# Inverse roots on ScalarE and GpSimd in place of GpSimd's power, and 175 more state products on GpSimd

## The chip, the cores and the metric

One core of one Trainium2 chip runs the whole program. The metric is device time in microseconds (us). The engines are called PE (TensorE, matrix products), PEld (its weight loads), DVE (VectorE), ACT (ScalarE), POOL (GpSimd) and SP (SyncE, which here only issues DMAs).

## The reference, cut to what matters

Eight images of 64 channels and 128 x 128 pixels go through two layers. The first is a filter of nine weights for each pixel, from a small convolution and a softmax. The second norms its input, runs two bidirectional selective-scan (Mamba) blocks over the 16,384 pixels as a sequence, multiplies the outcome with a convolved branch, norms again and ends in a gated feed-forward net (FFN). What the change touches are the norms and the scan:

```python
def layernorm(x, w, b):
    mu = x.mean(-1, keepdims=True)
    var = ((x - mu) ** 2).mean(-1, keepdims=True)
    return (x - mu) * jax.lax.rsqrt(var + EPS) * w + b

def rmsnorm(x, w):
    return x * jax.lax.rsqrt((x * x).mean(-1, keepdims=True) + EPS) * w

def selective_scan(u, dt, A, Bm, Cm, D, z):
    dt = jax.nn.softplus(dt)
    dA = jnp.exp(jnp.einsum('bdl,dn->bldn', dt, A))
    dBu = jnp.einsum('bdl,bnl,bdl->bldn', dt, Bm, u)
    ...                                    # h[l] = dA[l] * h[l-1] + dBu[l]
    y = jnp.einsum('bldn,bnl->bdl', hs, Cm) + D[None, :, None] * u
    return y * jax.nn.silu(z)
```

The state has 128 channels times 16 numbers, so 2048 rows of 16,384 steps for each direction of each block of each image.

## The kernel before, in words

The sequence is cut into chunks of 1024 steps: 16 chunks make a pass, and each image has four passes (two blocks, two directions), so there are 8 x 64 = 512 chunks. In each block the first direction is a **first pass** (it stores its output to DRAM) and the other a **second pass** (it adds the stored output, multiplies by the gate, projects, and norms the result for the next block). A chunk is 16 **steps**, u = 0 to 15; one step is one tile of 128 state rows by 1024.

In a step, ACT computes the decays `w` into PSUM (`decay`, L1097, two buffers), DVE scans them with the driving term `bu` (`scan`, L1115 and L1117), and the states are multiplied by `cp` to give `hs` (`product`). For an odd step this product is made by DVE (L1139); for an even one that `on_pool` names, DVE scans into `hs` directly and POOL multiplies in place (L1136). ACT copies the last column of the states for the next chunk (`keep`, L1129). POOL makes the driving terms two steps at a time (`drive`, L1089, three buffers) and one product for each chunk (`dtx`, L1045). PE sums the products over the state (`collect`, L1155). Softplus runs for a later chunk in step u = 2, Silu in step u = 11.

Beside the chunks run three other kinds of work on the same engines: the **front** (first layer and three norms of the next image, beside chunks 36 to 62 of an image), the **mix** (the convolved branch and a norm, beside chunk 62 and the first ten or so chunks of the next image) and the **FFN** (beside chunks 11 to 35 of the next image; three Gelus each in `gelus`, L853 and L855). "Plain" chunks have nothing beside them; they lie mostly in the first image. Before the first chunk stand two or so pieces of the first front alone, and after the last one a remainder of the last FFN.

A norm goes as follows. PE sums squares into 8 columns (`means`), ACT adds epsilon (`means_out`, L458), POOL raises to the power −0.5 (`root`, L461), PE spreads the result over the channels (`rb` in `spread`, L467), and DVE multiplies (`scaled`, `third_norm`, `normed`: L585, L617, L1201). There are 768 roots: three for each of 128 front pieces, one for each of 128 mix pieces, one for each of 256 second-pass chunks.

The order is written out by hand: `at(time, phase, function)` puts each piece of work at a step time and a phase (FEED, SCAN, MID, PROD, DECAY, REST), all are sorted by these two, and each engine takes its instructions in that order. The same phase keeps the order in which the pieces were planned: chunks first, then front, mix and FFN. For the norm that is:

```python
at(b + 13, DECAY, n.means_out)
at(b + 14, REST, n.root)
feed(b + 17, n.spread, mm_tile)
at(b + 18, DECAY, self.normed)
```

ACT holds one table of functions at a time. Exp, Silu, Softplus and Gelu need different ones; before the change each load stands directly ahead of the function that needs it.

Of the kernel before, what the change touches and what calls it, by code (L numbers as in the profile page):

```python
# [8 lines left out]
F32 = mybir.dt.float32  # L9
BF16 = mybir.dt.bfloat16  # L10
AF = mybir.ActivationFunctionType
ALU = mybir.AluOpType
# [3 lines left out]
P = 128  # L16
# [3 lines left out]
ROWS = 4  # L20
# [13 lines left out]
G = 4  # L34
U = G * G
PW = W + 2
FEED, SCAN, MID, PROD, DECAY, REST = range(6)

IMAGE = 4 * NT * U
# [16 lines left out]
def kernel(ctx: ExitStack, tc: tile.TileContext, a: dict, out: bass.AP):  # L56
# [6 lines left out]
    nc = tc.nc  # L63
# [8 lines left out]
    def const(shape, name, dt=F32):  # L72
        return wp.tile(shape, dt, tag=name, name=name)
# [3 lines left out]
    def dram(shape, name):  # L77
        return dramp.tile(shape, F32, tag=name, name=name + "_dram")


    def image(name):

        return dram([C, PW * PW + PW], name)

    def pixels(img):
        return img[:, 0 : PW * PW].rearrange("c (r w) -> c r w", w=PW)

    def clear(img, lo=0, hi=PW + 1):
        nc.sync.dma_start(
            img.rearrange("c (r w) -> c r w", w=PW)[:, lo:hi],  # L90
            zero.rearrange("c (o w) -> c o w", o=1).to_broadcast([C, hi - lo, PW]),
        )

    x_img, xm_img, xn_img = image("x"), image("xm"), image("xn")
    dw_img = [image(f"dw{i}") for i in range(2)]
    zero = const([C, PW], "zero")
    nc.vector.memset(zero, 0.0)
# [11 lines left out]
    nc.vector.tensor_tensor(center, center, ident, ALU.add)  # L109
    eps = const([P, 1], "eps")  # L110
    nc.vector.memset(eps, EPS)
    neg_half = const([P, 2 * ROWS], "neg_half")
    nc.vector.memset(neg_half, -0.5)

    sel_y = const([P, 32, 1], "sel_y")
    nc.vector.tensor_reduce(sel_y, ident.rearrange("k (m n) -> k m n", n=G), AX.X, ALU.add)
# [49 lines left out]
    for h in range(2):  # L166
        nc.sync.dma_start(b1[h * 32 : (h + 1) * 32, :], row(a["L0_conv_b1"]))
        nc.sync.dma_start(w2v[64:65, 9 * h : 9 * h + 9], a["L0_conv_b2"].rearrange("(o k) -> o k", o=1))


    FRONT_W, MIX_W, FFN_W = 6 * 32 + P, 12 * C, 18 * P + 2 * C + P + 2 * 9
    w_dram = [dram([P, n], f"w{i}") for i, n in enumerate((FRONT_W, MIX_W, FFN_W))]
# [210 lines left out]
    wk = ctx.enter_context(tc.tile_pool(name="wk", bufs=2))  # L383
# [19 lines left out]
    def tmp(name):  # L403
        return wk.tile([P, N], F32, tag="tmp", name=name, bufs=12)
# [41 lines left out]
    class Norm:  # L446
# [7 lines left out]
                )  # L454

        def means_out(self):
            self.r = wk.tile([P, 2 * ROWS], F32, tag="r", name="r", bufs=4)
            nc.scalar.activation(self.r, self.mp[:, 0 : 2 * ROWS], AF.Identity, bias=eps)  # L458

        def root(self):  # L460
            nc.gpsimd.tensor_tensor(self.r, self.r, neg_half, ALU.pow)  # L461

        def spread(self, ps):
            self.rb = ps("rb")
# [15 lines left out]
    class Front:  # L480
        def __init__(self, b, c):
            self.b, self.c, self.p = b, c, b % 2
            self.n1, self.n2, self.n3 = Norm(), Norm(), Norm()
            self.t, self.wbk, self.alone = {}, {}, False
# [278 lines left out]
    class Ffn:  # L763
# [84 lines left out]
        def gelus(self):  # L848
            if self.alone:
                nc.scalar.activation(self.gt, self.gt, AF.Gelu)  # L850
            else:
                self.gt = tmp("gt")
                nc.scalar.activation(self.gt, self.rest[0], AF.Gelu)  # L853
            for h in range(2):
                nc.scalar.activation(self.ga[h], self.ga[h], AF.Gelu)  # L855

        def rest_times(self):
            nc.vector.tensor_tensor(self.gt, self.gt, self.rest[1], ALU.mult)
# [33 lines left out]
        def plan(self, a):  # L892
            early = 12 if self.alone else 0
            at(a - 4 - early, REST, self.load, 0)
            at(a - 3 - early, REST, self.load, 1)

            if self.alone:
                at(a - 6, REST, self.before_taps)
                at(a - 5, DECAY, self.before_taps_out)
                at(a - 5, REST, self.taps, 0)  # L900
                at(a - 2, REST, self.taps, 1)
                groups = ((0, 0, self.first_out, 2), (3, 1, self.times, 6))
                gelus, out = 3, 9
            else:
                groups = ((0, 0, self.first_out, 5), (6, 2, None, 0), (14, 1, self.times, 19))
                gelus, out = GELU, 19
            for t, g, end, to in groups:
                for i in range(4):
                    at(a + t + (0 if self.alone else i), REST, self.conv, g, i)
                for h in range(2 if end else 0):  # L910
                    at(a + to, DECAY, end, h)
            at(a + gelus, REST, self.gelus)
            at(a + gelus + 2, MID, self.rest_times)
            at(a + out - 5, REST, self.load_x2)
            at(a + out, REST, self.project)
            at(a + out + 2, DECAY, self.add)
            at(a + out + 2, REST, self.store)

    def plan_ffn(b, a, step):
        at(a - (10 if step == LAST_FFN_STEP else 4), REST, load_weights, 2)  # L920
        for c in range(NCH):
            Ffn(b, c).plan(a + step * c)


    gelu_times = {IMAGE * b + FFN_AT + FFN_STEP * c + GELU for b in range(B - 1) for c in range(NCH)}
# [7 lines left out]
    class Chunk:  # L933


        def __init__(self, i):
            self.b, self.l, self.d, self.t, self.second = order[i]
            self.i, self.t0 = i, U * i
            self.first = i % NT == 0
            self.pairs = PAIRS[i % 2]  # L940
            r, last = self.t0 % IMAGE, self.b == B - 1
            self.beside_front = (
                FRONT_AT - FRONT_STEP <= r < FRONT_AT + NCH * FRONT_STEP + 16 and not last
            ) or self.t0 < FIRST_FRONT_AT + NCH * FRONT_STEP + 16
            self.beside_gelu = any(self.t0 - U <= t < self.t0 + 2 * U for t in gelu_times)
            self.prev = None
            self.bus, self.hss, self.ws = {}, {}, {}
            self.dup, self.dtp, self.bp, self.cp, self.yv = {}, {}, {}, {}, {}
            self.norm = Norm()
# [42 lines left out]
        def silu(self):  # L992
            nc.scalar.activation(self.xc, self.xc, AF.Silu)
            if self.second:
                nc.scalar.activation(self.gt, self.gt, AF.Silu)

        def store_gate(self):
            self.gt_d = sd.tile([DI, T], F32, tag="gate", name="gate_dram", bufs=4)
            nc.sync.dma_start(self.gt_d, self.gt)
            self.gt = {}  # L1000
# [18 lines left out]
        def softplus(self):  # L1019
            dt = self.dt  # L1020
            nc.scalar.activation(dt, dt, AF.Softplus)

        def bc(self):
            self.bcp = mm_tile("bcp")
            for i, s in enumerate(halves):
                nc.tensor.matmul(
                    self.bcp[32 * i : 32 * i + 32, :], wbc[:, self.l, self.d, :], self.xc[:, s],
                    start=True, stop=True,
                )
# [45 lines left out]
        def on_pool(self, u):  # L1075


            if u % 2 or u % 8 == 4 or self.t0 + u - 1 in gelu_times:
                return False
            return u != 8 or self.beside_front or self.beside_gelu  # L1080

        def over_pair(self, what, k):
# [217 lines left out]
    for b in range(B):  # L1300
# [2 lines left out]
        plan_mix(b, a + (LAST_MIX_AT if last else MIX_AT), LAST_MIX_STEP if last else MIX_STEP)  # L1303
        plan_ffn(b, a + (LAST_FFN_AT if last else FFN_AT), LAST_FFN_STEP if last else FFN_STEP)
    with tc.manual_schedule():
        for key in sorted(steps):
            for fn, args in steps[key]:
                fn(*args)
# [29 lines left out]
```

## Time and profile before

| what | value |
|---|---|
| three runs, median (lowest to highest) | 29515.6 us (29510.37 to 29532.13) |
| the profiled execution's own time | 29464.12 us |
| its span | 29462.3 us |
| POOL busy | 27653.4 us, 8732 instructions |
| DVE busy | 27280.7 us, 17559 instructions |
| ACT busy | 18566.1 us, 28357 instructions |
| PE busy | 23428.5 us, mean granted clock 0.866 |
| roots on POOL (L461) | 768, 1265.8 us |
| products on POOL (L1136) and on DVE (L1139) | 2832, 6693.9 us and 5360, 6562.4 us |

The profile takes one execution by the hardware profiler. Its groups give a line, an engine, an operation, output and inputs by the program's names, a count, the busy time and the mean duration of one, and then the idle time directly before these instructions with what ended it. A window gives each engine's busy time in a stretch of the span. The waits say which instruction waited for which, with total, number and longest.

### The profile page before, as it was taken

To read this page: it belongs to the slowest core of one execution; us is meant where nothing else is said; L and a number is where in the kernel's file an instruction comes from. 1 tells how busy PE (TensorE), PEld (TensorE's weight loads), DVE (VectorE), ACT (ScalarE), POOL (GpSimd) and SP (SyncE) were. 2 spreads that over 40 slices of the span, in tenths; PEclk is the share of its full clock that TensorE was granted. 3 is DMA by queue.
4 is the path that set the end of the run, shared out by engine and by line. 5 is a ranking of instruction groups with operands and counts; after the bars stand their busy time and mean duration, and the time that the engine had idled before them with its cause. 6 is when DMAs were issued, how large, how long until landed. Compare 5 with 4: busy or idle time off the path is not lost. (4 is left out here: it accounts for less than half of the span.)

```text
span 29462.3 us, 312607 instructions
## 1 busy us (share of the span) xinstructions
PE 23428.5 (80%) x97852; PEld 7363.8 (25%) x97852; DVE 27280.7 (93%) x17559; ACT 18566.1 (63%) x28357; POOL 27653.4 (94%) x8732
## 2 busy tenths in 40 slices
PE   7666888878788787887878878787787878878678
PEld 3211222223222232222322223222222222222123
DVE  4999999999999999999999999999999999999997
ACT  3666666666666666666666666666666666666663
POOL 3999999999999999999999999999999999999993
PEclk8777888988889888988889888898888988889789
DMA  4676677767777677776787767777677776777674
GB/s 114 221 245 219 226 246 242 240 217 230 249 241 237 216 234 254 239 233 217 235 256 235 233 219 237 251 239 229 221 239 247 236 228 219 246 246 238 217 250 142
DMA packets 2592281, 6762.83 MB, mean 230 GB/s; under 512 B 431270, under 2 KB 736822, under 8 KB 2589462
## 3 DMA queue, kind: packets, MB, share of 16 engines
q1 hardware_dynamic: 2590614, 6742.83, 70.7%
q8 instruction: 774, 12.68, 0.2%
q14 instruction: 893, 7.32, 0.1%
HBM read 5509.49 MB, written 1265.19 MB: 230 GB/s over the span
## 5 line engine op out<-in xcount | busy, mean ns | idle before, releaser
L1089 POOL TENSOR_TENSOR bu<-dup,bp 128x2048 f32<-128x2048 f32 x4096 | 18584.8, 4543 | 373.6 <-DVE w L1117 231.0
L1097 ACT ACTIVATE w<-dtp,a_neg 128x1024 f32<-128x1024 f32 x8192 | 9159.6, 1118 | 793.8 <-DVE hs L1115 334.7
L1136 POOL TENSOR_TENSOR hs<-hs,cp 128x1024 f32<-128x1024 f32 x2832 | 6693.9, 2364 | 236.0 <-ACT state L1129 183.1
L1139 DVE TENSOR_TENSOR hs<-w,cp 128x1024 f32<-128x1024 f32 x5360 | 6562.4, 1224 | 317.2 <-DMA cp<-bc_dram 88.5
L1117 DVE TENSOR_TENSOR_SCAN w<-w,state,bu 128x1024 f32<-128x1024 f32 x2683 | 6290.5, 2345 | 302.1 <-ACT w L1097 301.0
L1115 DVE TENSOR_TENSOR_SCAN w<-w,state,bu 128x1024 f32<-128x1024 f32 x2677 | 6278.7, 2345 | 250.2 <-ACT w L1097 248.8
L1155 PE MATMUL y<-hs,sel_y 128*32 128x512 f32 x32768 | 5126.6, 701 | 55.3 <-POOL hs L1136 55.1
L1129 ACT COPY state<-w 128x1 f32<-128x1 f32 x5360 | 838.0, 156 | 5484.9 <-DVE hs L1139 5433.5
L1117 DVE TENSOR_TENSOR_SCAN hs<-w,state,bu 128x1024 f32<-128x1024 f32 x1413 | 3308.4, 2341 | 183.3 <-issue 121.2
L1115 DVE TENSOR_TENSOR_SCAN hs<-w,state,bu 128x1024 f32<-128x1024 f32 x1419 | 3321.2, 2340 | 38.6 <-PE y L1155 17.5
L1148 PE MATMUL y<-xc,dskip 128*64 128x512 f32 x4096 | 1571.0, 856 | 1656.3 <-ACT yv L1172 1383.9
L967 PE MATMUL xp<-hn,wx 128*128 128x512 f32 x4096 | 2353.8, 704 | 653.6 <-ACT xc L973 476.2
L799 PE MATMUL fp<-fw,bgw 128*128 128x512 f32 (+1 forms) x5760 | 2272.1, 636 | 105.9 <-ACT ga L846 66.2
L1129 ACT COPY state<-hs 128x1 f32<-128x1 f32 x2832 | 541.2, 191 | 1937.8 <-DVE hs L1117 989.9
L1155 PEld LDWEIGHTS y<-hs,sel_y 128*32 128x32 f32 x32768 | 730.1, 117 | 3666.8 <-issue 2458.0
L1008 PE MATMUL dp<-xc,wdt 128*128 128x512 f32 x2048 | 1226.9, 683 | 463.8 <-ACT dt L1015 373.0
L461 POOL TENSOR_TENSOR r<-r,neg_half 128x8 f32<-128x8 f32 x768 | 1265.8, 1649 | 318.2 <-ACT r L458 299.2
L1097 ACT ACT_TABLE_LOAD x1134 | 1454.9, 1283 | 20.5
L566 PE MATMUL acc<-t,ident 128*128 128x512 f32 x2304 | 1370.9, 680 | 99.3 <-DVE hc L585 94.7
L805 PE MATMUL fp<-fw,bgw 64*128 64x512 f32 (+1 forms) x5760 | 1415.1, 609 | 0.0
L1045 POOL TENSOR_TENSOR dt<-dt,xc 128x1024 f32<-128x1024 f32 x512 | 1214.9, 2373 | 173.2 <-DMA dt_dram<-dt 154.7
L967 PEld LDWEIGHTS xp<-hn,wx 128*128 128x128 f32 x4096 | 830.6, 216 | 1967.7 <-issue 961.4
(211 smaller groups left out, 25729.1 us busy)
## 6 DMA issues: line engine op xcount, KB each, us to landing
bp<-bc_dram SPq DMA_DIRECT2D x4096, 256.0 KB
dup<-du_dram SPq DMA_DIRECT2D x4096, 256.0 KB
dtp<-dt_dram SPq DMA_DIRECT2D x4096, 256.0 KB
cp<-bc_dram SPq DMA_DIRECT2D x4096, 256.0 KB
hn<-hn_dram SPq DMA_DIRECT2D x1024, 256.5 KB
dt_dram<-dt SPq DMA_DIRECT2D x512, 512.0 KB
du_dram<-dt SPq DMA_DIRECT2D x512, 512.0 KB
yf_dram<-yv SPq DMA_DIRECT2D x512, 256.0 KB
```

The lines of the kernel that those rows point to most:

```text
L799: nc.tensor.matmul(o, wpair[:, i, g, m], self.win[h][:, i : i + ROWS, 0:W], start=(i == 0), stop=False)
L805: nc.tensor.matmul(o, wlast[rows, i, g, m], self.win[h][rows, i : i + ROWS, lo : W + lo], start=False, stop=(i == 2),)
L967: nc.tensor.matmul(self.xp[h], wx[:, self.l, self.d, i, :], self.hn2[:, s.start + 2 * i : s.stop + 2 * i], start=(i == 0), stop=(i == 1),)
L1089: nc.gpsimd.tensor_tensor(bu, self.dup[self.pairs[k][1]], self.over_pair("bp", k), ALU.mult)
L1097: nc.scalar.activation(w, self.dtp[gp][:, i, :], AF.Exp, scale=a_neg[:, self.l, self.d, g, j : j + 1])
L1115: nc.vector.tensor_tensor_scan(to, w, bu, s0, ALU.mult, ALU.add)
L1117: nc.vector.tensor_tensor_scan(to[:, ::-1], w[:, ::-1], bu[:, ::-1], s0, ALU.mult, ALU.add)
L1129: nc.scalar.copy(self.column(u), h[:, T - 1 : T] if self.d == 0 else h[:, 0:1])
L1136: nc.gpsimd.tensor_tensor(hs, hs, c, ALU.mult)
L1139: nc.vector.tensor_tensor(hs, w, c, ALU.mult)
L1148: nc.tensor.matmul(self.y[C * h : C * h + C, :], dskip[:, self.l, self.d, C * gp : C * gp + C], self.xc[:, s], start=True, stop=False,)
L1155: nc.tensor.matmul(self.y[lo : lo + 32, :], sel_y, hs[:, i, s], start=False, stop=(k % 4 == 3))
```

## The change

The mean of squares plus epsilon, v, is no longer raised to −0.5 by POOL. ACT computes r = exp(−0.5 ln v), v itself by Identity, and q = r squared. POOL makes one Newton step in three instructions, r (1.5 − 0.5 q v). So that Ln and Exp need no switch of tables between them, one table with both is loaded at the start and directly after every Silu, Softplus and (outside the last image) Gelu, rather than ahead of the next Exp. And `on_pool` names more steps: u = 4 in second-pass chunks beside a front, and in chunks beside an FFN without a Gelu directly ahead of u = 0 or 8.

```diff
+EXP_AND_LN = "natural_log_exp_and_others"
...
-    neg_half = const([P, 2 * ROWS], "neg_half")
-    nc.vector.memset(neg_half, -0.5)
...
+    def exp_and_ln():
+        nc.scalar.preload_act_table_set(EXP_AND_LN)
...
         def means_out(self):
-            self.r = wk.tile([P, 2 * ROWS], F32, tag="r", name="r", bufs=4)
-            nc.scalar.activation(self.r, self.mp[:, 0 : 2 * ROWS], AF.Identity, bias=eps)
+            mp, shape = self.mp[:, 0 : 2 * ROWS], [P, 2 * ROWS]
+            self.v, self.r, self.q = [wk.tile(shape, F32, tag=n, name=n, bufs=4) for n in ("rv", "r", "rq")]
+            nc.scalar.activation(self.r, mp, AF.Ln, bias=eps)
+            nc.scalar.activation(self.v, mp, AF.Identity, bias=eps)
+            nc.scalar.activation(self.r, self.r, AF.Exp, scale=-0.5)
+            nc.scalar.activation(self.q, self.r, AF.Square)

         def root(self):
-            nc.gpsimd.tensor_tensor(self.r, self.r, neg_half, ALU.pow)
+            nc.gpsimd.tensor_tensor(self.q, self.q, self.v, ALU.mult)
+            nc.gpsimd.tensor_scalar(self.q, self.q, -0.5, 1.5, ALU.mult, ALU.add)
+            nc.gpsimd.tensor_tensor(self.r, self.r, self.q, ALU.mult)
...
             for h in range(2):
                 nc.scalar.activation(self.ga[h], self.ga[h], AF.Gelu)
+            if not self.alone:
+                exp_and_ln()
...
+            self.skips = any(self.t0 + u - 1 in gelu_times for u in (0, 8))
...
             if self.second:
                 nc.scalar.activation(self.gt, self.gt, AF.Silu)
+            exp_and_ln()
...
             nc.scalar.activation(dt, dt, AF.Softplus)
+            exp_and_ln()
...
         def on_pool(self, u):
-            if u % 2 or u % 8 == 4 or self.t0 + u - 1 in gelu_times:
+            if u % 2 or u == 12 or self.t0 + u - 1 in gelu_times:
                 return False
+            if u == 4:
+                return self.beside_front and self.second or self.beside_gelu and not self.skips
             return u != 8 or self.beside_front or self.beside_gelu
...
     with tc.manual_schedule():
+        exp_and_ln()
         for key in sorted(steps):
```

## The prediction

> **What bounds the kernel now.** I read the busy line first, then windows over single stages, then who waits, then single instructions in time order.
>
> ```profile
> PE 23428.5 (80%) x97852; PEld 7363.8 (25%) x97852; DVE 27280.7 (93%) x17559; ACT 18566.1 (63%) x28357; POOL 27653.4 (94%) x8732
> ```
>
> DVE and POOL are both nearly full, ACT is not. An average over stages does not say which of the two ends a stage, so windows follow. Each row has start and end, length, then busy time of PE, PEld, DVE, ACT and POOL. Counting scans (16 to a chunk) the five hold 20 plain chunks, 12 first-pass chunks beside a front, 15 second-pass chunks beside a front, 10 beside a mix, 9 beside an FFN.
>
> ```profile
> 1436.00:2491.00 1055.00, 653.94 (x2445) 179.35 (x2448) 1022.46 (x589) 652.52 (x957) 1020.37 (x296) 0.77 0.74 240
> 2491.00:3172.00 681.00, 505.13 (x2107) 161.87 (x2111) 637.20 (x428) 429.47 (x678) 663.92 (x225) 0.82 0.65 212
> 3172.00:4043.00 871.00, 723.27 (x3291) 265.41 (x3284) 824.60 (x575) 575.12 (x920) 855.41 (x293) 0.89 0.73 235
> 4101.00:4650.00 549.00, 429.28 (x1857) 116.15 (x1856) 515.36 (x300) 343.95 (x514) 534.60 (x167) 0.86 0.79 253
> 5070.00:5573.00 503.00, 446.63 (x1812) 139.22 (x1810) 471.97 (x286) 330.93 (x489) 471.18 (x139) 0.92 0.72 240
> ```
>
> Beside a front POOL is busy 97.5% (663.92 of 681) and 98.2% (855.41 of 871), beside a mix 97.4%; DVE has 5 to 6% idle there. So **POOL sets the pace beside fronts and mixes**. In plain chunks both are at 97% and POOL waits for DVE, so DVE does. Beside an FFN both are at 94%: there bursts of ACT set it. The waits of POOL and DVE in the first front window:
>
> ```profile
> POOL r L461 <- ACT r L458: 10.0, 6, 2.4
> POOL hs L1136 <- ACT state L1129: 5.5, 8, 1.6
> DVE w L1117 <- ACT w L1097: 20.2, 11, 3.2
> DVE hn L617 <- PE rb L467: 10.0, 4, 2.9
> ```
>
> DVE waits for ACT's decays and for `rb`, the spread inverse root, which comes out of POOL. The groups that the change touches:
>
> ```profile
> L1136 POOL TENSOR_TENSOR hs<-hs,cp 128x1024 f32<-128x1024 f32 x2832 | 6693.9, 2364 | 236.0 <-ACT state L1129 183.1 <-DMA cp<-bc_dram 34.6 <-DVE hs L1139 5.0
> L1139 DVE TENSOR_TENSOR hs<-w,cp 128x1024 f32<-128x1024 f32 x5360 | 6562.4, 1224 | 317.2 <-DMA cp<-bc_dram 88.5 <-PE y L1155 5.0 <-DVE w L1117 1.8
> L461 POOL TENSOR_TENSOR r<-r,neg_half 128x8 f32<-128x8 f32 x768 | 1265.8, 1649 | 318.2 <-ACT r L458 299.2 <-ACT state L1129 16.6 <-DMA dup<-du_dram 1.3
> L538 POOL TENSOR_TENSOR lg<-lg,sp 128x72 f32<-128x72 f32 x256 | 84.1, 329 | 3.2 <-ACT sp L534 3.2
> L1097 ACT ACT_TABLE_LOAD x1134 | 1454.9, 1283 | 20.5
> ```
>
> The power on 8 elements takes 1649 ns where a subtraction of 72 takes 329: nearly all of it is the power.
>
> **What the skill says.** GPSIMD Engine Reference, Performance versus the Vector engine: an addition of 2048 takes 4497 ns on GpSimd and 2293 on VectorE. The trace's drive of 2048 agrees (4543 ns). The same page, Instruction dispatch: a GpSimd instruction that reads its predecessor's output needs a wait on the completion semaphore. The three new ones form such a chain; no run here shows its price. ScalarE: Activation LUTs, Table sets: the natural-log set holds both exp and ln, so the new functions need no switch beside the decays; What ACT_TABLE_LOAD costs: 1283 ns, and a drain of 1380 for every switch. The trace has the 1283, but only 20.5 us of idle before 1134 loads: no such drain.
>
> **The change, part by part.**
>
> 1. *Root on POOL.* In time order a power starts at 6860.12 and the next instruction at 6861.72, so it holds POOL 1.60 us. Three small instructions replace it. Between 1024 elements (2364 ns) and 72 (329) the slope is 2.14 ns an element, so 8 elements are an estimated 0.19 us: 0.57 for three. Against the usual overlap of 0.05 stand two waits for the predecessor. Lower bound 0.45 (all overlap), upper 1.2 (0.33 each and 0.1 a wait). I take 0.62: **0.98 us saved a root**, with both ends kept.
>
> 2. *Means on ACT.* One activation (L458, mean 261 ns) becomes four, two of them waiting for the one before. An independent one follows L458 after 0.17 us (6861.20 to 6861.37); the dependent two are an estimated 0.24 each. The chain is about 0.85, **0.6 longer**, 0.3 to 0.8 at the bounds. 768 times this is 460 us on an engine 37% idle, so as work it costs nothing (all of it, were that idle time gone). As delay it counts where POOL already stands waiting. From the start times of L461 and ends of L458, the power follows within 0.8 us in 82 of 159 roots of first-pass front chunks, in 78 of 308 of second-pass ones, 21 of 92 of first-pass mix chunks. Elsewhere POOL is inside a drive, which hides it. Behind the waiting POOL stand the next drive and product; behind the longer ACT chain the next `state` copy and decay, for which DVE waits; its slack there is a scan of 2.3 us less 1.3 of copy and decay, so 0.6 fits.
>
> 3. *Products.* Evaluating the new rule for all 512 chunks, u = 4 moves to POOL in 175: 105 second-pass front chunks and 70 beside an FFN. POOL gains 2.31 us each (6867.80 to the next start, 6870.11), DVE loses 1.14 (6881.11 to 6882.25), its scan going to `hs` at the same 2.34.
>
> 4. *Table loads.* The instruction orders count 2273 before and 2274 after: only their place moves, to directly after Silu, Softplus and Gelu. ACT around a Softplus:
>
> ```profile
> 6880.19 1.06 ACT L1021 ACTIVATE dt<-dt 128x1024 f32<-128x1024 f32 x1
> 6882.37 0.16 ACT L1129 COPY state<-w 128x1 f32<-128x1 f32 x1 [1.12 <-DVE hs L1139]
> 6882.42 0.73 ACT L1204 ACTIVATE hn<-hn,v_normf_w 128x512 f32<-128x512 f32 x1
> 6883.17 1.28 ACT L1097 ACT_TABLE_LOAD   x1
> 6884.46 1.12 ACT L1097 ACTIVATE w<-dtp,a_neg 128x1024 f32<-128x1024 f32 x1
> ```
>
> The load now falls into the 1.12 us of waiting, and this decay, which the scan after u = 4 needs, comes about 1.1 us earlier: what DVE loses as cover there, ACT gains. Where ACT doesn't wait, nothing changes. I count zero; a gain is possible, a loss only where the delayed `state` copy is late, and after these functions the copy is of an odd or DVE step, which no POOL product needs.
>
> Nothing is added on PE or SP (same counts of instructions, no DMA); dropping the constant costs nothing.
>
> *Sum over stages.* Roots and chunks are counted from L461 in the chunks of each kind.
> - First-pass front, 97 chunks, 159 roots: −0.98 × 159 + 0.6 × 82 = −107 on POOL. Next late is DVE: 637 busy and 38 of waits make 675 of 681 us in the window, and of these waits only the 10 for `rb` shrink with POOL. That caps the gain at 0.5 to 1.3 us a chunk; I take −90.
> - Second-pass front, 105 chunks, 308 roots: −302 + 47 + 2.31 × 105 = −12.
> - First-pass mix and plain, 89 chunks, 92 roots: −90 + 13; the plain ones are DVE's, so −60.
> - First-pass beside FFN with the product, 35 chunks, 21 roots: +81 − 21. In the window 4651 to 4753, where this begins, POOL is busy all 102 us, so most shows: +45.
> - Second-pass beside FFN with it, 35: POOL has 3.3 of 53 us idle (5186 to 5239), which covers +1.3; DVE is relieved: −15.
> - The rest (77 + 35 beside Gelus, 39 second-pass plain or mix): 0, since DVE or ACT sets them.
>
> Together −132. The profiled execution took 29464.1 us (span 29462.3), 51.5 below the median of the three runs, 29515.6. So 29464 − 132 = 29332 on its scale and **29,385 on the median's** (29383.5, rounded).
>
> **Rivals.**
> - *Slower: the chain of three costs more than it saves room for.* In the POOL-bound stages 580 roots pay for 140 products (324 us) and 109 us of new waiting; that needs 433 / 580 = 0.75 us saved a root, so it turns if the three hold POOL over 0.85 us. At 1.0 the sum is −348 + 433 = +85: 29,600; at 1.2 about 29,700. For it: no dependent pair of this size in the trace. Against it: 64x18 memsets take 0.11.
> - *No change:* second-pass fronts give back what first-pass ones win, because ACT's extra 460 us delays decays and DVE's wait for `w` (550 us over the run) grows by a third. 29,515. Against it: ACT idle mostly waits for DVE's product (5433 us before `state`).
> - *Faster still:* three at 0.45 and no added wait: −1.15 × 580 + 324 = −343, so 29,175. For it: the earlier table loads shorten decays. Against: in second-pass fronts POOL stays full.
> - That the change isn't made as described is excluded by the orders: no load was added before a decay.
>
> **Numbers.** The measurement can tell about 0.2% (59 us). My case 0.45, faster still 0.17, no change 0.13, slower 0.25. The range 29,180 to 29,640 leaves out the ends of the outer two.
>
> **What would show it.** In the profile after: three small groups on POOL summing to 0.5 to 0.7 us where L461 had 1.65; POOL busy lower by about 350 us (753 less 404), DVE by 200; ACT up by some 460; first-pass front chunks (56.7 us now) about 0.9 shorter, second-pass ones (58.1) about equal. I am wrong if the three sum above 0.85, if POOL's wait for ACT's root input rises far above 300 us, or if DVE's wait for `w` grows past 700.

## Result, and the profile after

The changed kernel takes 29594.7 us (median of 11 runs, 29581.1 to 29632.8) against 29513.1 for the kernel before (11 runs, 29497.7 to 29532.1). The ratio is 1.0030, 95% interval 1.0022 to 1.0038: **slower by 0.3%, some 82 us**. The profiled execution took 29581.1 us (span 29579.4), 117 more than that of before. The forecast was 29,385, faster; the value lies in the range, the direction was wrong.

The page of the kernel after, its busy line and three of its groups (count, then busy time, mean ns, idle time before and what ended it):

```profile
PE 23448.9 (79%) x97852; PEld 7336.3 (25%) x97852; DVE 27094.1 (92%) x17383; ACT 18942.7 (64%) x30662; POOL 27278.6 (92%) x10443
...
L1153 POOL TENSOR_TENSOR hs<-hs,cp 128x1024 f32<-128x1024 f32 x3007 | 7093.2, 2359 | 369.0 <-ACT state L1146 283.9
L1156 DVE TENSOR_TENSOR hs<-w,cp 128x1024 f32<-128x1024 f32 x5185 | 6348.2, 1224 | 335.8 <-DMA cp<-bc_dram 117.1
...
L172 ACT ACT_TABLE_LOAD x1137 | 1458.8, 1283 | 20.7 <-PEq L1345 0.7
```

POOL is busy 375 us less, DVE 187 less, ACT 376 more, and 175 products have changed engine (3007 − 2832). The work moved as foreseen; both full engines have less of it, and the program takes longer.

Windows of the kernel after over the same five stretches of chunks as before (length, then PE, PEld, DVE, ACT, POOL busy):

```profile
1449.80:2508.50 1058.70, 662.66 (x2440) 180.27 (x2432) 1022.81 (x589) 662.20 (x1006) 1003.94 (x328) 0.76 0.75 239
2508.50:3185.10 676.60, 503.40 (x2108) 158.73 (x2111) 636.95 (x428) 438.61 (x735) 645.21 (x263) 0.83 0.65 214
3185.10:4056.20 871.10, 721.88 (x3289) 259.67 (x3281) 807.96 (x561) 592.84 (x1052) 845.58 (x392) 0.89 0.74 234
4117.20:4662.70 545.50, 425.45 (x1861) 113.59 (x1864) 515.57 (x298) 350.12 (x553) 521.50 (x193) 0.87 0.81 255
5090.90:5593.10 502.20, 448.46 (x1808) 139.84 (x1806) 468.82 (x284) 337.71 (x516) 468.51 (x160) 0.92 0.72 238
```

In the second row (first-pass front) POOL has lost 18.7 us of work (663.9 to 645.2), the stretch only 4.4; in the third POOL lost 9.8 and DVE 16.6, the stretch nothing. Over all eight images it is less still. Taking each chunk from its first scan to the next chunk's, the 97 first-pass front chunks average 56.99 us (before 56.74), with POOL busy 54.09 in each (before 55.45): **POOL was freed by 1.36 us a chunk, and the chunk became no shorter.**

Where the 117 us lie is told by the same starts of chunks, summed over the eight images by position in the image, as a difference to before (one profile each; kernels that are alike in a stretch differ by some 20 us there; the few us ahead of the first chunk, in chunk 63 and after the last one are left out):

| us against before | chunks 0–10, mix | 11–35, FFN | 36–47, first-pass front | 48–62, second-pass front |
|---|---|---|---|---|
| after | +17 | **+84** | +19 | −17 |
| loads_only | +11 | **+60** | +1 | −6 |
| roots_only | +14 | +37 | +10 | −43 |
| products_only | −2 | +48 | +5 | **+124** |
| act_longer | −2 | +26 | +19 | +9 |
| roots_late_loads | +6 | −17 | −12 | +15 |
| power_twice | +126 | +83 | +112 | **+429** |
| products_front2 | +35 | +40 | +6 | −10 |
| products_ffn2 | +8 | +36 | +15 | −60 |
| roots_softplus_ln2 | −31 | −2 | −31 | −25 |

Most of the profile's loss is beside the FFN, which the forecast had at +30 in all. The rows of the other kernels are read below. No part of the change by itself reaches the +84: the roots with early loads have +37, and +36 when the FFN's products are added. A share of it may be chance of one execution: DVE waited 117 us for the transfers of `cp` here, 73 in the profile of products_ffn2.

The new groups on POOL, and those on ACT:

```profile
L469 POOL TENSOR_TENSOR rq<-rq,rv 128x8 f32<-128x8 f32 x768 | 161.7, 211 | 442.1 <-ACT rq L465 358.3 <-ACT state L1146 83.6
L471 POOL TENSOR_TENSOR r<-r,rq 128x8 f32<-128x8 f32 x768 | 156.9, 204 | 63.9
L470 POOL TENSOR_SCALAR rq<-rq 128x8 f32<-128x8 f32 x768 | 151.9, 198 | 67.2
```

```profile
L463 ACT ACTIVATE rv<-ms,eps 128x8 f32<-128x8 f32 x768 | 203.4, 265 | 0.0
L462 ACT ACTIVATE r<-ms,eps 128x8 f32<-128x8 f32 x768 | 202.0, 263 | 58.6 <-PE ms L455 58.5
L464 ACT ACTIVATE r<-r 128x8 f32<-128x8 f32 x768 | 162.7, 212 | 0.0
L465 ACT ACTIVATE rq<-r 128x8 f32<-128x8 f32 x768 | 160.3, 209 | 24.3
```

The three on POOL sum to 613 ns; the idle time ahead of the second and third (67.2 and 63.9 us over 768) adds 0.087 and 0.083, so the trio holds POOL **0.78 us**. Its wait for the root's input is 442 us where the power's was 318.

### The profile page after: what moved, and what is told of

It reads as the page before. It is cut to its first block, busy times and chain, and to the rows that moved or that the text cites. A ratio compares the mean times of both kernels' runs of the same rounds, so it can differ in the third digit from the quotient of the medians.

```text
span 29579.4 us, 315677 instructions
## 1 busy us (share of the span) xinstructions
PE 23448.9 (79%) x97852; PEld 7336.3 (25%) x97852; DVE 27094.1 (92%) x17383; ACT 18942.7 (64%) x30662; POOL 27278.6 (92%) x10443
## 5 line engine op out<-in xcount | busy, mean ns | idle before, releaser
L1153 POOL TENSOR_TENSOR hs<-hs,cp 128x1024 f32<-128x1024 f32 x3007 | 7093.2, 2359 | 369.0 <-ACT state L1146 283.9
L1156 DVE TENSOR_TENSOR hs<-w,cp 128x1024 f32<-128x1024 f32 x5185 | 6348.2, 1224 | 335.8 <-DMA cp<-bc_dram 117.1
L1134 DVE TENSOR_TENSOR_SCAN w<-w,state,bu 128x1024 f32<-128x1024 f32 x2634 | 6175.6, 2345 | 309.8 <-ACT w L1114 302.6
L1132 DVE TENSOR_TENSOR_SCAN w<-w,state,bu 128x1024 f32<-128x1024 f32 x2551 | 5981.9, 2345 | 303.7 <-ACT w L1114 300.3
L1172 PE MATMUL y<-hs,sel_y 128*32 128x512 f32 x32768 | 5208.1, 712 | 144.6 <-POOL hs L1153 144.4
L1132 DVE TENSOR_TENSOR_SCAN hs<-w,state,bu 128x1024 f32<-128x1024 f32 x1545 | 3616.1, 2341 | 92.2 <-ACT state L1146 57.1
L1134 DVE TENSOR_TENSOR_SCAN hs<-w,state,bu 128x1024 f32<-128x1024 f32 x1462 | 3423.4, 2342 | 280.4 <-issue 148.2
L172 ACT ACT_TABLE_LOAD x1137 | 1458.8, 1283 | 20.7 <-PEq L1345 0.7
L986 ACT ACTIVATE xc<-xp,cbias 128x512 f32<-128x512 f32 x1024 | 696.0, 680 | 926.6 <-PE xp L980 922.7
```

Of the source, the lines that this page charges most:

```text
L172: nc.scalar.preload_act_table_set(EXP_AND_LN)
L1132: nc.vector.tensor_tensor_scan(to, w, bu, s0, ALU.mult, ALU.add)
L1134: nc.vector.tensor_tensor_scan(to[:, ::-1], w[:, ::-1], bu[:, ::-1], s0, ALU.mult, ALU.add)
L1153: nc.gpsimd.tensor_tensor(hs, hs, c, ALU.mult)
L1156: nc.vector.tensor_tensor(hs, w, c, ALU.mult)
L1172: nc.tensor.matmul(self.y[lo : lo + 32, :], sel_y, hs[:, i, s], start=False, stop=(k % 4 == 3))
```

## Experiments

Each is compared with runs of the kernel before on the same chip; ratios carry their 95% interval. Kernels that ran beside different runs of the kernel before are compared by their ratios. (The numbered theories in the texts recorded before each run are set out in the first of them.) Two theories are followed here: **A**, the forecast's slower rival, the trio costs POOL more room than it leaves; **B**, POOL isn't the bound in most stages, so that its relief buys little, and what is put on ACT's path (the longer chain, the earlier loads) and the moved products cost what they cost.

### The parts by themselves

The change is taken apart. roots_only has the new roots and early loads; products_only the new `on_pool` with the power kept; loads_only the early loads alone.

```diff
roots_only = after, but:
-            if u % 2 or u == 12 or self.t0 + u - 1 in gelu_times:
-            ...
+            if u % 2 or u % 8 == 4 or self.t0 + u - 1 in gelu_times:
products_only = before, with after's on_pool and self.skips
loads_only = before, and:
+            exp_and_ln()      # after Silu, Softplus, Gelu, and once at the start
```

> The changed kernel with the old rule of on_pool: the new roots and the early table loads, no product moved. Theory 1 (GpSimd sets the pace beside fronts and mixes, and what was lost is the 175 products): with the chain of three at about 0.75 us a root, GpSimd gains 0.85 x 580 roots in the stages that it paces, less some waiting; 200 to 400 us faster than before. Theory 2 (the pace is set by decays, states and matrix products that wait for each other, so GpSimd's relief is worth nothing, and ScalarE's chain, longer by 0.6 us a root, is in that loop): no faster, 0 to 80 us slower. Theory 3 (the whole loss is the moved products): equal to before within 30 us.

> The kernel before with the new rule of on_pool: 175 products move from VectorE to GpSimd, roots stay the power on GpSimd, table loads stay where they were. Theory 1: GpSimd, which sets the pace there, gets 2.31 us more in 140 chunks: 200 to 320 us slower. Theory 2: VectorE's relief of 1.14 us is given back as a wait for decays or for the buffers of hs, and GpSimd is nearly full: 0 to 100 us slower. Theory 3: it carries the whole loss, 60 to 120 us slower.

> The kernel before with the table that holds exp and ln loaded directly after Silu, Softplus and Gelu, and nothing else changed. Theory 1 and 3: within 30 us of before. Theory 2: a decay after a Softplus comes up to 1.1 us earlier where ScalarE waited for VectorE, so 0 to 60 us faster; if the state copies that now stand behind the load are in the loop, 0 to 60 us slower.

Measured: **roots_only 1.0007** (0.9998 to 1.0015), **products_only 1.0059** (1.0046 to 1.0071), **loads_only 1.0020** (1.0013 to 1.0026); medians 29486.8, 29645.6 and 29528.2 against 29471.1. The roots, which take 775 us of work from POOL (27653.4 to 26878.2), gain nothing that can be measured; the 200 to 400 us that theory 1 expected of them are excluded. The products put on the old kernel cost 174 us, between theory 3 (up to 120) and theory 1 (from 200). And the loads, which had been counted at zero, cost 57.

The trace of the kernel before has 2273 table loads: 1134 ahead of decays, 512 each ahead of Silu and Softplus, nearly all others ahead of Gelu. Where an early one of them can cost: one case is a wait of PE (line waited for: us in total, times, longest us), in the kernel before and in loads_only:

```profile
PE y L1148 <- ACT yv L1172: 1383.9, 410, 14.9
```

```profile
PE y L1157 <- ACT yv L1181: 1669.3, 466, 14.2
```

PE waits 285 us more for ACT to copy the finished `y` out of PSUM: in a first-pass chunk that copy stands, in ACT's order, behind the load that now follows Softplus at once. The runs divide cleanly: with early loads this wait is 1623 to 1694 us (six kernels), with late ones 1305 to 1413 (eight). The other case is Gelu. ACT in time order around one `gelus`, before and in loads_only:

```profile
5244.57 1.14 ACT L855 ACTIVATE ga<-ga 128x512 f32<-128x512 f32 x2
5245.61 0.15 ACT L1129 COPY state<-w 128x1 f32<-128x1 f32 x1
5245.78 1.28 ACT L1097 ACT_TABLE_LOAD   x1
5247.08 1.12 ACT L1097 ACTIVATE w<-dtp,a_neg 128x1024 f32<-128x1024 f32 x1
```

```profile
5258.01 1.14 ACT L860 ACTIVATE ga<-ga 128x512 f32<-128x512 f32 x2
5259.16 1.28 ACT L174 ACT_TABLE_LOAD   x1
5260.46 0.16 ACT L1138 COPY state<-w 128x1 f32<-128x1 f32 x1
5260.65 1.12 ACT L1106 ACTIVATE w<-dtp,a_neg 128x1024 f32<-128x1024 f32 x1
```

Before, the `state` copy overlapped Gelu's end and the decay began 1.37 us after it (5245.71 to 5247.08). With the load in between the copy is 1.4 us later and the decay begins 1.50 us after Gelu (5259.15 to 5260.65): ACT wasn't waiting there, so the load saves nothing, and the copy is late. The column for chunks 11–35, where the Gelus are, holds +60 of this kernel's loss. How the 57 us divide between these two cases wasn't measured, and neither is shown to be the cause: roots_only has the longer wait of PE too (1658 us), and stands only some 13 us above the same kernel with late loads (next section but one).

### No Newton step

```diff
-            nc.scalar.activation(self.v, mp, AF.Identity, bias=eps)
-            nc.scalar.activation(self.q, self.r, AF.Square)
...
-            nc.gpsimd.tensor_tensor(self.q, self.q, self.v, ALU.mult)
-            nc.gpsimd.tensor_scalar(self.q, self.q, -0.5, 1.5, ALU.mult, ALU.add)
-            nc.gpsimd.tensor_tensor(self.r, self.r, self.q, ALU.mult)
```

> The new roots without the Newton step (left out: v, q and the three instructions on GpSimd; r is exp(-0.5 ln v) as ScalarE gives it), early table loads, old rule of on_pool. GpSimd is relieved of 1.6 us a root, ScalarE's chain is longer by one activation, some 0.2 us. Theory 1: 580 x 1.6 us, up to what VectorE then allows: 150 to 500 us faster than before. Theory 2: roots come earlier, but GpSimd's relief itself is worth nothing: within 60 us of before, and faster than roots_only by what the shorter chain on ScalarE is worth (0 to 80 us).

Measured: **1.0003** (0.9995 to 1.0011), median 29477.2, beside 1.0007 for roots_only. With the trio gone altogether, the last 0.78 us a root and two of the four activations, the median is 10 us lower, which is within the intervals. A trio that took too much room would have shown here: theory A falls. So do the 150 to 500 us that theory 1 expected.

### Late loads, a longer chain on ACT, and more work on POOL

Four kernels, on one chip. In two, the natural-log table is loaded ahead of the first Exp or Ln that needs it, as before the change. act_longer keeps the power and gives `means_out` four activations in a row; power_twice raises the root to the power 1 once more on POOL.

```diff
roots_late_loads, no_newton_late_loads:
-            exp_and_ln()               # after Silu, Softplus, Gelu
+            exp_and_ln()               # in means_out, exps, decay, unless it is held
act_longer:
+            nc.scalar.activation(t, self.mp[:, 0 : 2 * ROWS], AF.Identity, bias=eps)
             nc.scalar.activation(self.r, self.mp[:, 0 : 2 * ROWS], AF.Identity, bias=eps)
+            nc.scalar.activation(self.r, self.r, AF.Identity)
+            nc.scalar.activation(self.r, self.r, AF.Identity)
power_twice:
             nc.gpsimd.tensor_tensor(self.r, self.r, neg_half, ALU.pow)
+            nc.gpsimd.tensor_tensor(self.r, self.r, one, ALU.pow)
```

> roots_only with each load of the exp-and-ln table ahead of the first Exp or Ln that needs it, where it stood before the change, rather than directly after Silu, Softplus and Gelu. Theory 2a (two small effects stand against each other: the early loads cost what loads_only showed, 57 us, and the roots themselves are worth 40 to 50): 40 to 50 us faster than before. Theory 2b (roots and loads don't add up: ScalarE's longer chain costs what GpSimd's relief brings, and the order of loads doesn't matter beside it): within 20 us of roots_only, so 0 to 35 us slower than before.

> no_newton (the Newton step left out) with the late loads. Theory 2a: 45 to 60 us faster than before. Theory 2b: within 20 us of no_newton.

> The kernel before, where the mean goes through four activations in a row on ScalarE (a second copy, then two more that wait for the one before) ahead of the unchanged power on GpSimd: ScalarE's longer chain, by some 0.6 us a root, alone. If the longer chain is in the loop beside fronts: 60 to 150 us slower. If it is hidden in ScalarE's idle time: within 30 us of before.

> The kernel before with a second power (to the exponent 1) on GpSimd after each: 768 x 1.6 us more on GpSimd, 1230 us, and nothing else changed. If GpSimd is far from the pace: within 100 us of before. If GpSimd stands at a knee, where relief is worth nothing and load costs in full beside fronts (467 of the 768 roots): 500 to 900 us slower. Theory 1 said the same of this side, but also that relief gains, which roots_only and no_newton did not show.

Measured, against 29469.8: roots_late_loads **1.0002** (0.9994 to 1.0010), no_newton_late_loads **0.9995** (0.9986 to 1.0003), act_longer **1.0015** (1.0007 to 1.0024), power_twice **1.0258** (1.0244 to 1.0272).

The longer chain alone costs 44 us, between what the two expectations had. With a chain as long and 775 us less on POOL the time is that of before (+3), so the relief is worth about 40 us, give or take 35 by the intervals: a nineteenth of the work removed. That value is a difference of two kernels and supposes that the parts add. The loads show that parts need not: alone the early ones cost 57 us, together with the new roots some 13 (1.0007 against 1.0002), which the intervals can't tell from nothing. So theory 2a, by which these two kernels had to be 40 to 60 us faster than before, didn't come true. In the other direction POOL's work is dear: 1230 us more (28883.0) cost 755. **POOL stands at a knee: below today's load it hardly counts, above it more than half of each microsecond shows.** Which side a stage is on is to be seen in who waits. DVE's waits over the whole run, first of the kernel before, then of power_twice, then of the kernel after:

```profile
DVE w L1117 <- ACT w L1097: 301.0, 256, 3.2
DVE hc L585 <- PE rb L467: 254.1, 106, 12.8
```

```profile
DVE hc L588 <- PE rb L470: 878.0, 310, 13.4
```

```profile
DVE w L1134 <- ACT w L1114: 302.6, 262, 3.2
DVE w L1132 <- ACT w L1114: 300.3, 241, 3.9
DVE hc L595 <- PE rb L477: 296.1, 154, 12.7
```

Where POOL sets the pace, DVE stands at `hc`, which needs `rb`, the root that comes late out of POOL's queue: 878 us with two powers. In the kernel before it was 254 over 29,462, and only 21 of these lie in the 105 second-pass front chunks and under 2 in the 97 first-pass ones; with two powers it is 420 and 166. That is the mark that was missing there. (DVE's waits for `rb` at `hn`, 160 and 136 us before, are no such mark: they are 146 and 140 with two powers.) The busy share hardly tells the two apart: in this window of power_twice over the second-pass fronts (columns as above) POOL is at 99.5%,

```profile
3238.10:4169.40 931.30, 731.21 (x3283) 267.35 (x3284) 826.87 (x576) 576.08 (x920) 926.22 (x336) 0.87 0.68 221
```

against 98.2% for the same chunks before.

### The products, split, and Softplus in the held table

Two kernels have the new roots and one half of the new products each. The other two take a switch of tables away: Softplus as ln(1 + exp x), whose two functions are in the table that is held, so that the loads fall from 2274 to 1250. One has only the new roots, the other the whole change; both load late.

```diff
products_front2:
-                return self.beside_front and self.second or self.beside_gelu and not self.skips
+                return self.beside_front and self.second
products_ffn2:
+                return self.beside_gelu and not self.skips and not self.beside_front
roots_softplus_ln2, all_softplus_ln2:
-            nc.scalar.activation(dt, dt, AF.Softplus)
+            exp_and_ln()
+            nc.scalar.activation(dt, dt, AF.Exp)
+            nc.scalar.activation(dt, dt, AF.Ln, bias=1.0)
```

> The changed kernel with only the 105 moved products of second-pass front chunks. The whole change stands about 0.2% (60 to 70 us) above roots_only. If the moved products are given back as waits for ScalarE after the Softplus of u = 2, a second-pass front chunk has yv of VectorE as cover there (0.68 us) and loses little: 0 to 40 us above roots_only. If GpSimd's fill decides (it is fuller there than beside an FFN): 40 to 70 us above it.

> The changed kernel with only the 70 moved products beside an FFN. By waits after Softplus (VectorE's scans of u = 5 and 6 waited 0.8 to 1.2 us longer there in the changed kernel's trace, which is as much as the product took): 20 to 60 us above roots_only. By GpSimd's fill: within 30 us of roots_only.

> roots_late_loads with Softplus computed as ln(1 + exp(x)), both from the table that is already held: two activations of 1.06 us in place of one and of two table loads of 1.28, 1.5 us less on ScalarE in each chunk, in one burst. If ScalarE's bursts set the pace together with VectorE: 100 to 500 us faster than roots_late_loads. If VectorE alone sets it, or waits for the matrix products: within 60 us of it.

> The whole change, with late loads and Softplus as ln(1 + exp(x)). If the moved products lose because VectorE's product at u = 4 was cover for the burst of the Softplus at u = 2, this version gains from them with the burst shortened: 0 to 100 us faster than roots_softplus_ln. If they lose for another reason (GpSimd's fill, buffers of hs that the matrix products free late): 40 to 100 us slower than roots_softplus_ln, as without it.

Measured, against 29468.7: products_front2 **1.0019** (1.0012 to 1.0025), products_ffn2 **1.0009** (1.0002 to 1.0015), roots_softplus_ln2 **0.9967** (0.9954 to 0.9979), all_softplus_ln2 **0.9982** (0.9975 to 0.9989).

Beside roots_only (1.0007) the 105 products of the second-pass fronts cost about 0.12%, 35 us; the 70 beside the FFN 0.02%, which can't be told from nothing; all 175 some 0.23%. The fronts' part is hardly more than its interval, the whole is clear of it. The halves don't add up to the whole, and the intervals leave that open. With Softplus out of its table the products still cost 37 us (29415.0 less 29378.3), where a gain was expected if they had only lost the cover of the burst at Softplus. So that burst isn't the reason, or not alone.

In the second-pass fronts the waits point to POOL again. DVE's wait at `hc` over the whole run, in roots_only and in products_front2:

```profile
DVE hc L595 <- PE rb L477: 258.1, 113, 13.0
```

```profile
DVE hc L595 <- PE rb L477: 319.9, 160, 13.1
```

Taken from the traces for the 105 second-pass front chunks alone, DVE's idle time ahead of `hc` is, in us:

| before | roots_only | products_ffn2 | products_front2 | after | products_only | power_twice |
|---|---|---|---|---|---|---|
| 21 | 9 | 9 | 51 | 53 | 121 | 420 |

The relief by the roots takes the 21 to 9; the products, 2.3 us more on POOL in each of these chunks, take it to 51. The 42 us between are about what the products cost there. In products_only, with the power still on POOL, they cost most. DVE's idle time in these chunks grew at other places too, by 0.35 us a chunk ahead of the scans into `w` and 0.30 at `t`, while it lost 1.15 us of work; so this is the largest single part, not a proof.

Beside the FFN the products gained nothing either, though DVE had less to do. Why is seen in a second-pass chunk of the kernel after where u = 4 went to POOL (in time order: start, length, engine and line, idle time before and what ended it):

```profile
5220.08 2.34 DVE L1134 TENSOR_TENSOR_SCAN hs<-w,state,bu 128x1024 f32<-128x1024 f32 x1
5220.22 2.08 PE L1201 MATMUL op<-yv,wo 128*128 128x512 f32 x2 [3.70 <-DVE yv L1187]
...
5225.27 1.06 PE L1172 MATMUL y<-hs,sel_y 128*32 128x512 f32 x8
...
5226.51 2.35 DVE L1134 TENSOR_TENSOR_SCAN hs<-w,state,bu 128x1024 f32<-128x1024 f32 x1 [0.33 <-PE y L1172]
```

A buffer of `hs` holds the states of two steps, and there are three. The scan of u = 6 writes into the one that steps 0 and 1 had, and PE frees that one when it has summed them (`y<-hs`, done at 5226.33). In PE's list this sum stands behind the projection, which had waited 3.70 us for `yv`. Over the 35 chunks of this kind the sum ends 20.5 us into the chunk (20.2 before) and the scan of u = 6 starts at 20.7, as before. DVE, without the product of u = 4, is there earlier and waits: its idle time ahead of this scan rose from 0.18 to 1.19 us a chunk, which gives back the 1.00 us of work that DVE lost there (50.24 to 49.24). In the 35 first-pass chunks the wait is elsewhere: ahead of the scan of u = 5, for a decay of ACT after the Softplus, DVE's idle time rose from 0.00 to 0.86 us. The product had been cover for other engines' work. This is read from the order and the times; no run tried it by itself.

roots_softplus_ln2 is the fastest of all, 90 us below the kernel before (five runs). From roots_late_loads (1.0002) it differs in Softplus alone, which is thus worth some 100 us, give or take 45; from 100 was expected if ACT's bursts set the pace with DVE, up to 60 if not. Its busy line:

```profile
PE 23333.3 (79%) x97852; PEld 7326.7 (25%) x97852; DVE 27279.1 (93%) x17558; ACT 18072.1 (62%) x30150; POOL 26879.7 (91%) x10268
```

DVE has as much to do as before (27280.7) and ends sooner: the gain is time in which DVE had stood idle. Against roots_late_loads its waits for `w` fell from 553 to 508 us and those at `hc` from 256 to 213. ACT, with a lower share than PE, DVE and POOL, has 827 us less of work than in roots_late_loads (18899.1), and that brought more by the medians than the 775 us taken from POOL, which brought about 40; the intervals of the two gains still touch, and the clock may have a share in the first (last section).

## Why the prediction was wrong, point by point

- **"POOL sets the pace beside fronts and mixes": the step that failed.** It was read from busy shares of 97 to 98%. That DVE waited for POOL was read from `rb`, with 10 us in a window of 681. The runs: with 775 us less on POOL and late loads the time is that of before (1.0002), and with no work of the roots left on POOL it hardly moves (0.9995). The sum then turned POOL's relief into time, stage by stage:

| stage | forecast, us | measured, us |
|---|---|---|
| first-pass front | −90 | +24 |
| second-pass front | −12 | −16 |
| first-pass mix and plain | −60 | +14 |
| first-pass beside FFN, with the product | +45 | +17 |
| second-pass beside FFN, with the product | −15 | +4 |
| the rest | 0 | +66 |

  (Measured: 97 × (56.99 − 56.74), and so on, from the starts of chunks; +8 more lie ahead of the first and after the last chunk.) The two rows that were to bring 150 us brought a loss of 38. The second row is right by luck: its terms were −255 for the roots and +243 for the products, and roots_only has −43 there, products_front2 33 more than that. The waits that were shown pointed to the error in the first row: 38 us of DVE's waits in 681, of which 10 were for `rb`. DVE's own stream of scans and products, with its waits for ACT and PE, makes the pace there.
- **Trio on POOL.** Forecast 0.62 us, bounds 0.45 and 1.2; it is 0.78. The instructions are nearly as estimated (0.61 for three, 0.57 estimated), and each wait for the predecessor adds 0.085 where 0.05 had been allowed for both. The Trainium skill's GPSIMD Engine Reference, section Instruction dispatch, asks for a wait on the producer's semaphore where a GpSimd instruction reads partitions that a different core of the engine wrote in the one before. Whether these three are such a case no run here shows; the runs give the price of the gaps that stand between them. At 0.78 it is under the 0.85 from which the slower rival decides. That rival's number, 29,600, lies 5 us from the outcome, but **its mechanism didn't act**: without any trio the time is the same.
- **Means on ACT, "as work it costs nothing".** The chain's delay was priced as 109 us of POOL's waiting (measured 442 less 318, so +124), and as nothing for ACT's other customers. act_longer shows +44 us for such a chain without any relief of POOL, so "0.6 fits" in DVE's slack was too kind. The busy time, +376 where 460 was forecast, was the lesser miss.
- **Table loads, "I count zero".** +57 us on the old kernel, some 13 beside the new roots. The argument looked at the one Softplus where ACT was waiting. The loss that it named, a late `state` copy, was judged harmless because no POOL product needs it; after Gelu it is late by 1.4 us, and a second customer, PE's wait for `yv`, wasn't looked at. Which of them costs is open.
- **Products.** They were priced as POOL's gain of 2.31 us each, +243 in the fronts, and the rows beside the FFN at +45 and −15. The runs show 35 us for the fronts, next to nothing for the FFN, and about 65 together on top of roots_only. That DVE would only meet other waits earlier, PE's freeing of `hs` and ACT's decay, was in neither sum; the relief of DVE (187 us) is nowhere seen as time gained.
- **Right in the amounts of work:** POOL −375 (about −350), DVE −187 (−200), no drain at the switches of tables (20.7 us idle before 1137 loads), no instruction added on PE.
- **No change**, the rival, named DVE's wait for `w` as what would take the gain back. It grew from 550 to 603 us (301.0 and 248.8 to 302.6 and 300.3), a tenth where a third was named; and there was no gain to take.
- **The signs of being wrong that were named** didn't come, or only in part: the trio is under 0.85, the wait for `w` under 700, and POOL's wait for ACT's root input went from 299 to 358 us. None of them asks whether POOL sets the pace.

What stays open: why the relief of POOL shows in the second-pass fronts with early loads (−43) and not with late ones (+15), why early loads cost less beside the new roots, and why the two halves of the products cost less than the whole.

## To carry to other kernels

An engine at 98% is a suspect, not the bound: look for the instruction on another engine that waits for it, and if that wait is small beside the stage, its relief will buy next to nothing while more work on it can still cost dearly. Taking work from a busy engine gains nothing if its next instruction then waits for another engine: ask what the work had covered. Moving a function's table load ahead can cost; each copy and decay that now stands behind it has a customer to be asked. An engine with a low share whose results the busiest engine waits for can be worth relieving first: here two table switches a chunk taken from ACT were the only edit that clearly gained.

## What the runs showed of the hardware that was not expected

- A GpSimd instruction on 128x8 elements takes 198 to 211 ns, a dependent successor starts 0.085 us after it; the power takes 1637 to 1649 ns, eight times as much.
- An activation on 128x8 takes 263 to 265 ns where it reads the means that PE left in PSUM and a bias from a tile (L462, L463) and 209 to 212 where it reads ACT's own result and no bias tile (L464, L465). Which of the two makes the difference no run separates; a copy of one column takes 156 ns from `w` in PSUM and 191 from `hs` in SBUF, so PSUM isn't slower to read there. One that waits for its predecessor on ACT follows with almost no gap (24.3 us over 768 for L465).
- Exp and Ln on 1024 elements cost as much each as Softplus (1057 and 1043 ns against 1057). Here a second function in the held table was thus cheaper than the two loads of 1283 ns, there and back, that a table of its own needs.
- The mean granted clock of PE goes with the kernel: 0.867 for the runs of before, 0.864 for after and loads_only, 0.869 for act_longer, 0.871 for roots_softplus_ln2. Within the runs of a kernel 0.001 less went with some 9 us more (fit over 293 runs, correlation −0.53). If that is cause and not effect, 24 of the 57 us of loads_only, 45 of the 90 of roots_softplus_ln2 and some 20 of the 82 of the change itself are the clock's. Against it: no_newton has 0.864 and takes 6 us more than before, act_longer 0.869 and 44 more. No run separates it.
